# A graph layer and a mixture of experts on one core: where PSUM tiles share a bank, and the order of the work behind the edges

## The chip, the core and the metric

The kernel runs on one core of a Trainium2 chip. The core has a matrix engine (TensorE, PE in the rows; PEld is its weight load), a vector engine (VectorE, DVE), an activation engine (ScalarE, ACT), GpSimd (POOL), which here issues the indirect transfers, and SyncE (SP), which issues most other transfers. Each has its own instruction sequence and runs it in order; semaphores tie the sequences together. Matrix products land in PSUM, which is divided into banks; the framework gives each PSUM tile, and each buffer of a tile, a bank of its own. The metric is the time of one execution on the device, in microseconds.

## What is computed

There are 6250 nodes with 256 features and 100000 edges, sorted by their destination; the destinations are drawn so that low node numbers have many edges and high ones few. Everything is float32. Cut to what matters:

```python
x0 = layernorm(x); xn = layer_norm(x0, ln1_g, ln1_b)
h = (xn @ W).reshape(N, 8, 32)                   # 8 heads
e = leaky_relu(a_src[src] + a_dst[dst], 0.2)     # per edge (and self loop) and head
alpha = softmax of e over the edges of each destination
agg = segment_sum(h[src] * alpha, dst)
o = layer_norm(agg + xn @ W_res + bias, ln2_g, ln2_b)
x = x + o + (gelu_tanh(o @ ffn_w1 + ffn_b1) @ ffn_w2 + ffn_b2)     # 256 -> 1024 -> 256
t = layernorm(x)
# mixture of experts: 8 experts, each token goes to its best 2
w, idx = top-2 of softmax(t @ Wr + br), renormalised
y_e = gelu((norm(t) * ln_g[e] + ln_b[e]) @ W1[e] + b1[e]) @ W2[e] + b2[e]
x = x + sum over the 2 of w * y_e
```

## The kernel before

**First stage (to about 144 us).** Tiles of 128 nodes are normalised and turned, and give a table `tab_s` in DRAM (rows of `h` and two exponentials per head), tables of destination factors, and the accumulators `acc_lo` and `acc_hi` in SBUF. In this stage L724 writes the PSUM tile `ph` of 288 columns; L726 copies its first 256 columns on ACT into `hg`, and L727 adds a row to the last 32 on DVE into `abp`.

**Edge steps.** The edges are cut into 196 steps of 4 x 128 edges (`G` = 4). The steps run from the highest destinations to the lowest. A group of 1 to 8 steps shares a window of destinations; at high destinations a group is one step. What a step does is spread over seven places by `STAGES` (L922); the number is how many steps after the gather it is done, and the list's order is the order in which one step's work is issued: sum_up 6, weigh 3, add_tiles 4, place 4, turn_spread 1, give 2, spread 0, add_nodes 5, fetch 0. That is:

- fetch (POOL, L824): four gathers of rows of `tab_s` into `gs`, four buffers.
- spread (DVE, L833): one-hot rows `oh`; turn_spread (PE L846 into the tile `pt`, ACT L848): its transpose `oht`.
- give (PE L854): the factors of each edge's destination into `pz`, a tile of 64 columns with two buffers.
- weigh (DVE L862, L865, L866): `ww` is `gs` times `pz`, then the messages `msg`.
- add_tiles (PE L881): messages into `pl`; behind a group's last step ACT copies it to `part` (L885).
- add_nodes (PE L906, once a group): `part` into `p2`, a tile with one buffer; sum_up (DVE L917, twice): `p2` into `acc_lo` or `acc_hi`.

**Tasks between them.** All other work is written as tasks (L928 on): a function, an engine, a cost, tasks that it depends on with a gap in steps (1 step by default), and a PSUM tile that it takes and that a later task frees. The tasks stand in the list `pending`. In each step `run_tasks` (L949) goes through that list in order, again and again, and issues each task whose dependencies are met and whose engine has room left in that step: `ROOM` while there are edges (less what the edges take), `ROOM_AFTER` behind them. The order of all instructions is so fixed when the program is built; the waits between engines are then added by the framework from the tiles that the instructions read and write. The one tile `py` is held by one user at a time (the set `held`).

- first_product (L1157): `xn @ W_res` into `py`; add_biases (L1167, L1170) on DVE; stored to DRAM as `res_d` and `xp_d`.
- A node unit (L1193) is two tiles of 128 nodes: load_nodes (L1038, from `res_d` and `xp_d` into `res` and `xin`), divide, two norms, a net (next point), take_up (L1083), norm_new, store_new (L1106, SP), make_normed (L1119, ACT), logits (PE L1127 into `py`), choose (DVE L1135 on).
- A net (L1008): turn (PE L978 into `pt`, ACT L985 into `turned_in`); eight tasks up (L989), one for each 128 of the 1024 columns of the first layer: four matmuls (L993; a product of two halves of 128, each issued as two) into `ph`, a tile of 256 columns with two buffers, then the activation `ht` (ACT L996); then the tasks down (L999), up to 32 matmuls (L1003) into `py`.
- Each two node units make a chunk: mark, weight, count (PE L1286, L1287 into `py`), rank, enlist (all the expert blocks that are sure by now), scatter (POOL L1396: each token's row into `xs`, twice).
- Behind the chunk before the last, eight tasks clear (L1405, SP) write three rows of zeros per partition behind each expert's tokens, at a row that is read from `endi`. The framework puts them in order with each other and with the scatters, since all write `xs`.
- An expert block (L1504, L1521) is 256 rows of `xs` of one expert: load_weights (SP L1447 to L1449, 2 MB into two or three buffers), load_block (SP L1456), a net, finish (DVE L1488), weigh_block (ACT L1494), give_back (POOL L1498: an indirect transfer that adds to `out`, one for each 128 rows). There are 53 in the main loop: 50 whole and 3 half ones (numbers 50 to 52); `turn_of` is the order in which they run.

Of the kernel before, what the change touches and what calls it, by code (L numbers as in the profile page):

```python
# [45 lines left out]
F32 = mybir.dt.float32  # L46
# [8 lines left out]
P = 128  # L55
# [6 lines left out]
G = 4  # L62
# [7 lines left out]
BEHIND = {"PE": 0.5, "DVE": 1.4}  # L70
ROOM_AFTER = {"PE": 7.7, "DVE": 7.0, "ACT": 7.0, "POOL": 5.2, "SP": 1e9}

# [150 lines left out]
def gnn_moe_kernel(  # L223
# [28 lines left out]
    nc = tc.nc  # L252
# [10 lines left out]
    DA = D + H  # L263
# [42 lines left out]
    for i in range(NS - NF):  # L306
        turn_of += [NF + i, NF - (NS - NF) + i]
    turn_of += range(NS, NX)
# [483 lines left out]
    bps = edges.enter_context(tc.tile_pool(name="bps", bufs=1, space=PSUM))  # L792
    right = ctx.enter_context(ExitStack())

# [56 lines left out]
    def give(s):  # L851

        pz = bps.tile([P, G * 2 * H], F32, name="pz", bufs=2)
        nc.tensor.matmul(pz, live.pop((s, "oht")), live[order[s][0], "qd"].rearrange(  # L854
            "p j c -> p (j c)"), start=True, stop=True)
        live[s, "pz"] = pz
# [45 lines left out]
    @behind_group  # L902
    def add_nodes(q):
        part, oh2 = live.pop((q, "part")), live.pop((q, "oh2"))
        p2 = bps.tile([P, DA], F32, name="p2")
        nc.tensor.matmul(p2, oh2, part, start=True, stop=True)  # L906
        live[q, "p2"] = p2
# [32 lines left out]

    pending = []
    held = set()

    def task(*a, **k):
        t = Task(*a, **k)
        pending.append(t)
        return t

    def run_tasks(s, room):  # L949

        more = True
        while more:
            more = False
            for t in list(pending):
                if (t.take in held or room[t.eng] <= 0.0
                        or any(d.step is None or d.step + gap > s for d, gap in t.deps)):
                    continue
                pending.remove(t)
                t.step = s
                room[t.eng] -= t.cost  # L960
                if t.take:
                    held.add(t.take)
                if t.free:
                    held.remove(t.free)
                t.fn()
                more = True
# [22 lines left out]
    def up(c, env, w1, func, b):  # L989
        W = env["n"] * P  # L990
        ph = cps.tile([P, 2 * P], F32, name="ph", bufs=2)
        for k in range(KD):
            nc.tensor.matmul(ph[:, :W], w1[:, k, c * P:(c + 1) * P], env["in"][:, k, :W],  # L993
                             start=k == 0, stop=k == KD - 1)
        ht = cw.tile([P, 2 * P], F32, name="ht", bufs=2 * KF)
        nc.scalar.activation(ht[:, :W], ph[:, :W], func, bias=b[:, c:c + 1], scale=1.0)  # L996
        env["ht", c] = ht

    def down(j, c0, c1, env, w2):  # L999
        if j == 0 and c0 == 0:  # L1000
            env["py"] = cps.tile([P, 2, D], F32, name="py")
        for c in range(c0, c1):
            nc.tensor.matmul(env["py"][:, j, :], env["ht", c][:, j * P:(j + 1) * P], w2[:, c, :],  # L1003
                             start=c == 0, stop=c == KF - 1)

    turns, downs_, ups_ = [], [], []

    def net(env, src, deps, w1, w2, func, b, more=(), scale=None):  # L1008

        n = env["n"]  # L1010
        tn = task(lambda: turn(src(), "in", env, scale and scale()), "PE", 0.3 * n,
                  [*deps, *[(d, 0) for d in back(ups_, 2)]])
        free = [(d, 0) for d in back(downs_, 2)]
        ups = [task(lambda c=c: up(c, env, w1(), func, b()), "PE", 0.46 * n, [tn, *more, *free])
               for c in range(KF)]
        dn = []
        for j in range(n):
            for c in (0, KF // 2):
                dn.append(task(lambda j=j, c=c: down(j, c, c + KF // 2, env, w2()), "PE", 1.85,
                               [(dn[-1], 0)] if dn else [ups[-1]], take=None if dn else "py"))  # L1020
        turns.append(tn)
        ups_.append(ups[-1])
        downs_.append(dn[-1])
        return dn[-1]
# [98 lines left out]
    def logits(n, env):  # L1123
        pl = cps.tile([P, 2, D], F32, name="py")
        for j in range(n):
# [31 lines left out]
    def first_product(n, env):  # L1157
        py = cps.tile([P, 2, D], F32, name="py")
        for j in range(n):
# [21 lines left out]
    def first_unit(u):  # L1181
# [3 lines left out]
                                [(d, 0) for d in back(firsts, 2)]))  # L1185
        pr = task(lambda: first_product(n, env), "PE", 0.95 * n, [(first_loads[-1], 2)], take="py")
        ab = task(lambda: add_biases(n, env), "DVE", 0.7 * n,
                  [pr, *[(d, 0) for d in back(firsts, 1)]], free="py")
        firsts.append(task(lambda: store_first(t0, n, env), "SP", 0.0, [ab]))

    loads, turned, added, normed, chosen_, scattered = [], [], [], [], [], []

    def node_unit(u):  # L1193
        t0, n, _ = units[u]
        env = {"n": n}
        ld = task(lambda: load_nodes(t0, n, env), "SP", 0.0,
                  [(firsts[u], 0),
                   *[(d, 0) for d in back(turned, 2) + back(added, 2) + back(normed, 3)]])
        dv = task(lambda: divide(t0, n, env), "DVE", 0.85 * n, [ld])
        no = task(lambda: norm_out(n, env), "DVE", 0.6 * n + 1.9, [dv])  # L1200
# [4 lines left out]
                 scale=lambda: prm[:, PR_L2G:PR_L2G + 2 * KD])  # L1205
        tk = task(lambda: take_up(t0, n, env), "DVE", 0.35 * n, [dn, ao], free="py")
        nn = task(lambda: norm_new(t0, n, env), "DVE", 0.6 * n + 2.6,
                  [tk, *[(d, 0) for d in back(chosen_, 3)]])
        st = task(lambda: store_new(t0, n, env), "SP", 0.0, [tk])
        free = scattered[u - 4] + scattered[u - 3] if u >= 4 and u % 2 == 0 else []  # L1210
        mn = task(lambda: make_normed(n, env, u), "ACT", 0.55 * n,
                  [nn, (st, 0), *[(d, 0) for d in free]])
        tn = task(lambda: turn(env["xe"], "rt", env), "PE", 0.3 * n,
                  [mn, *[(d, 0) for d in back(chosen_, 2)]])
        lo = task(lambda: logits(n, env), "PE", 0.9 * n, [tn], take="py")
        ch = task(lambda: choose(t0, n, env), "DVE", 0.65 * n, [lo], free="py")
        loads.append(ld)
        turned.append(turns[-1])
# [64 lines left out]
    def count(env):  # L1283
        pr = cps.tile([P, 2, D], F32, name="py")
        m = env["m"].rearrange("p e t -> p (e t)")
# [102 lines left out]

    placed = {u: [] for u in range(NT)}
    between = cp.tile([P, 1], F32, name="between")  # L1390

    def scatter(u, j):
        t = units[u][0] + j
        n = rows(t)
        for k in range(2):
# [3 lines left out]
            tc.add_to_no_dep_group("slots", st.ins)  # L1399
            placed[u].append(st.ins)  # L1400
            tc.declare_no_dep(st.ins, group="slots", reason="each token has slots of its own")

            nc.gpsimd.memset(between, 0.0)

    def clear(e):  # L1405

        r = nc.sync.value_load(endi[0:1, e:e + 1], min_val=0, max_val=E * CAP - 3 * P)
        nc.sync.dma_start(xs[bass.ds(r, 3 * P), :].rearrange("(p r) d -> p r d", r=3),
                          blank[:, None, :].to_broadcast([P, 3, DX]))

    def chunk_tasks(us, final, before_final):
# [4 lines left out]
        ad = task(lambda: append(t0, n, env, us[0] // 2), "DVE", 1.0, [we])  # L1416
        co = task(lambda: count(env), "PE", 0.6, [mk], take="py")
        rk = task(lambda: rank(t0, n, env), "DVE", 2.6, [co], free="py")
        tok0 = chunked[0]
# [9 lines left out]
        for u in us:  # L1429
            scattered.append([task(lambda u=u, j=j: scatter(u, j), "POOL", 2.6,  # L1430
                                   [rk, ad, *[(d, 0) for d in cleared]])
                              for j in range(units[u][1])])
            sc += scattered[-1]
# [87 lines left out]
    def block_unit(b, env):  # L1521
# [6 lines left out]
        fi = task(lambda: finish(env), "DVE", 0.35 * n, [dn, *[(d, 0) for d in back(stored, 3)]],  # L1528
                  free="py")
        wb_ = task(lambda: weigh_block(env), "ACT", 0.45 * n, [fi, no])  # L1530
# [20 lines left out]
    final_list, there = [], None  # L1551
    s, u, since, was_nodes = 0, 0, [], False

    with tc.manual_schedule():
        nc.sync.dma_start(xs[E * CAP:, :].rearrange("(p r) d -> p r d", r=2),
                          blank[:, None, :].to_broadcast([P, 2, DX]))
        while s < NG + LASTST or pending or u < len(units) or len(blocks) < NS:
# [22 lines left out]
            while sum(t.cost for t in pending if t.eng == "PE") < QUEUE:  # L1580
                if (u < len(units) and units[u][2] <= s - LASTST
                        and not (ahead and was_nodes)):
                    was_nodes = True
                    node_unit(u)
                    since.append(u)
                    u += 1
                    if u % 2 == 0 or u == len(units):
                        chunk_tasks(since, u == len(units), u == len(units) - 1)
                        since = []
                elif ahead:  # L1590
                    was_nodes = False
# [54 lines left out]
```

## Time and profile before

| | |
|---|---|
| median of three runs | 1924.65 us (1918.36 to 1925.77) |
| the profiled execution | 1919.82 us; span of its instructions 1917.9 us |
| mean granted clock of PE over the span | 0.924 |
| busy: PE / DVE / ACT / POOL | 1614.6 / 1080.1 / 700.6 / 1124.8 us |
| moved by DMA | 347.86 MB, 181 GB/s on average |
| the two first-layer groups of L993 (experts, nodes) | 1696 and 800 matmuls, 386.5 and 194.1 us |
| ACT L996 (experts, nodes) | 424 and 200 activations, mean 468 and 470 ns |

How to read it. The page gives each engine's busy time, a strip of 40 slices of the span, a chain of work that ended last, and groups of like instructions with their busy time, the mean length of one and what ended the idle time in front of them. A row of a timeline is: start in us, length in us, engine, line, operation, what is written and read, how many; in brackets the idle time before it and what ended it. A row of waits reads "who waits <- for whom: us in total, times, longest". Matmuls run into each other, so a mean length of one (381 ns) is longer than the distance of two (about 218 ns, from 32 in 6.99 us).

### The profile page before, as it was taken

What the parts mean: (1) busy time and instruction counts of PE and PEld (TensorE: products, weight loads), DVE (VectorE), ACT (ScalarE), POOL (GpSimd) and SP (SyncE); (2) the same over time, 40 slices, a digit from 0 to 9 for tenths busy, and PEclk for the clock granted to TensorE, in tenths of its full rate; (3) what the DMA queues carried; (4) which work ended last, traced back from release to release, by engine and by line L of the source; (5) the groups of instructions that cost most, each with busy time, mean ns of one, the idle gap of its engine ahead of it and who ended that gap; (6) DMA issues with size and microseconds to landing.
All of it is one profiled execution on the core that took longest, in us unless ns stands there. A gap on an engine that the chain in (4) does not pass through costs nothing. (4 is left out here: it accounts for less than half of the span.)

```text
span 1917.9 us, 28185 instructions
## 1 busy us (share of the span) xinstructions
PE 1614.6 (84%) x8479; PEld 1238.1 (65%) x8479; DVE 1080.1 (56%) x3972; ACT 700.6 (37%) x1585; POOL 1124.8 (59%) x1162
## 2 busy tenths in 40 slices
PE   4835787878777899999799999999999996898996
PEld 3523565655555677776577777767777774676885
DVE  8836888877788757584755665546444351131010
ACT  3831233223222344344334434343434341442342
POOL 2027775755565767767677677777877772221222
PEclk8967899988877899999999999999999997998998
DMA  4967665554445476666565666767578674737671
GB/s 127 296 204 221 202 197 151 161 160 135 140 134 167 139 211 172 169 199 166 160 189 155 204 193 178 230 181 237 178 226 251 182 210 151 234 72 236 185 223 31
DMA packets 246622, 347.86 MB, mean 181 GB/s; under 512 B 46033, under 2 KB 202865, under 8 KB 246460
## 3 DMA queue, kind: packets, MB, share of 16 engines
q1 hardware_dynamic: 184268, 203.16, 32.7%
q0 software_dynamic: 58880, 139.32, 28.1%
q10 hardware_dynamic: 3312, 3.48, 0.6%
q8 instruction: 70, 1.15, 0.2%
q14 instruction: 92, 0.75, 0.1%
HBM read 282.50 MB, written 67.26 MB: 182 GB/s over the span
## 5 line engine op out<-in xcount | busy, mean ns | idle before, releaser
L824 POOL DMA_INDIRECT gs<-tab_s,srce x784 | 816.5, 1041 | 371.0 <-issue 201.6
L993 PE MATMUL ph<-turned_in,w1b 128*128 128x256 f32 (+1 forms) x1696 | 386.5, 381 | 35.0 <-DMA w1b<-in_L_ffn_W_dram 19.2
L1003 PE MATMUL py<-w2b,ht 128*128 128x256 f32 x1648 | 375.0, 386 | 14.3 <-DVE lg L1135 7.3
L993 PEld LDWEIGHTS ph<-turned_in,w1b 128*128 128x128 f32 x1696 | 300.5, 192 | 99.6 <-ACT ht L996 32.5
L1003 PEld LDWEIGHTS py<-w2b,ht 128*128 128x128 f32 x1648 | 316.1, 194 | 59.7 <-DVE lg L1135 8.9
L1498 POOL DMA_INDIRECT out_dram<-yb,tos x103 | 171.9, 1669 | 245.4 <-ACT yb L1494 125.3
L996 ACT ACTIVATE ht<-ph,pc 128x256 f32<-128x256 f32 (+1 forms) x424 | 196.5, 468 | 257.7 <-PE ph L993 255.5
L866 DVE TENSOR_TENSOR msg<-gs,msg 128x1024 f32<-128x1024 f32 x196 | 240.3, 1226 | 6.7
L993 PE MATMUL ph<-turned_in,w_sb 128*128 128x256 f32 (+1 forms) x800 | 194.1, 396 | 11.9 <-ACT ht L996 11.3
L1003 PE MATMUL py<-w_sb,ht 128*128 128x256 f32 x784 | 187.7, 400 | 11.2 <-DVE lg L1135 10.5
L1488 DVE TENSOR_TENSOR yb<-py,b2b 128x512 f32<-128x512 f32 (+1 forms) x53 | 35.8, 675 | 266.5 <-PE py L1003 252.9
L1003 PEld LDWEIGHTS py<-w_sb,ht 128*128 128x128 f32 x784 | 156.6, 202 | 38.9 <-DVE lg L1135 14.7
L993 PEld LDWEIGHTS ph<-turned_in,w_sb 128*128 128x128 f32 x800 | 151.7, 201 | 42.7 <-ACT ht L996 16.2
L848 ACT ACTIVATE oht<-pt 128x128 f32<-128x128 f32 x196 | 53.9, 275 | 288.5 <-PE pt L846 257.5
L885 ACT ACTIVATE part<-pl 128x264 f32<-128x264 f32 x110 | 42.9, 390 | 313.3 <-PE pl L881 310.3
L996 ACT ACTIVATE ht<-ph,prm 128x256 f32<-128x256 f32 (+1 forms) x200 | 92.8, 470 | 124.7 <-PE ph L993 124.4
L1396 POOL DMA_INDIRECT xs<-xe,slot x98 | 104.8, 1069 | 56.7 <-DMA xs<-blank 28.0
L881 PE MATMUL pl<-msg,oh 128*32 128x264 f32 x1568 | 131.1, 406 | 5.1 <-DVE msg L866 5.0
L906 PE MATMUL p<-part,oh 128*128 128x264 f32 x220 | 85.0, 472 | 55.3 <-DVE acc_hi L917 37.1
L862 DVE TENSOR_TENSOR ww<-gs,pz 128x64 f32<-128x64 f32 x196 | 42.1, 215 | 158.5 <-PE pz L854 100.3
L846 PEld LDWEIGHTS pt<-ident,oh 128*128 128x128 f32 x196 | 27.7, 141 | 139.0 <-issue 85.0
L917 DVE SCALAR_TENSOR_TENSOR acc_lo<-p,here,acc_lo 128x264 f32 x112 | 55.2, 493 | 101.1 <-PE p L906 79.6
(334 smaller groups left out, 1925.7 us busy)
## 6 DMA issues: line engine op xcount, KB each, us to landing
w1b<-in_L_ffn_W_dram SPq DMA_DIRECT2D x53, 1024.0 KB
w2b<-in_L_ffn_W_dram SPq DMA_DIRECT2D x53, 1024.0 KB
xb<-xs SPq DMA_DIRECT2D x50, 260.0 KB
gs<-tab_s,srce POOLq DMA_INDIRECT x784, 3.5
b2b<-in_L_ffn_b_dram SPq DMA_DIRECT2D x53, 128.0 KB
tab_s<-hg SPq DMA_DIRECT2D x12, 544.0 KB
xg<-in_x_dram SPq DMA_DIRECT2D x12, 512.0 KB
xt_d<-xt SPq DMA_DIRECT2D x12, 512.0 KB
```

Of the source, the lines that this page charges most:

```text
L824: nc.gpsimd.indirect_dma_start(out=gs[:, j, :], out_offset=None, in_=tab_s, in_offset=bass.IndirectOffsetOnAxis(ap=srce[:, t:t + 1], axis=0))
L848: nc.scalar.activation(oht, po[:, 0, :P], AF.Copy)
L866: nc.vector.tensor_tensor(msg[:, :, :D].rearrange("p t (h d) -> p t h d", h=H), gs[:, :, :D].rearrange("p t (h d) -> p t h d", h=H), msg[: ...
L881: nc.tensor.matmul(pl[j * W32:(j + 1) * W32, :], oh[:, j, :], msg[:, j, :], start=i == 0, stop=last)
L885: nc.scalar.activation(part, pl, AF.Copy)
L906: nc.tensor.matmul(p2, oh2, part, start=True, stop=True)
L917: nc.vector.scalar_tensor_tensor(to, p2, here[:, b, q:q + 1], to, op0=ALU.mult, op1=ALU.add)
L993: nc.tensor.matmul(ph[:, :W], w1[:, k, c * P:(c + 1) * P], env["in"][:, k, :W], start=k == 0, stop=k == KD - 1)
L996: nc.scalar.activation(ht[:, :W], ph[:, :W], func, bias=b[:, c:c + 1], scale=1.0)
L1003: nc.tensor.matmul(env["py"][:, j, :], env["ht", c][:, j * P:(j + 1) * P], w2[:, c, :], start=c == 0, stop=c == KF - 1)
L1396: st = nc.gpsimd.indirect_dma_start(out=xs, out_offset=bass.IndirectOffsetOnAxis(ap=slots[k][:n, t:t + 1], axis=0), in_=xes[u // 2][:n, pl ...
L1498: st = nc.gpsimd.indirect_dma_start(out=out, out_offset=bass.IndirectOffsetOnAxis(ap=tos[:, b, j:j + 1], axis=0), in_=env["yb"][:, j, :], ...
```

## The change

- `ROOM_AFTER`, the room of a step behind the edges, is halved.
- In `turn_of` each half block now comes behind a whole one in place of before it, so that the last block is a half one.
- `pz` is no longer a tile with two buffers but one half, by turns, of one tile `pzs`, and `ph` likewise of one tile `phs`. Each pair so lies in one bank, where it had two.
- `p2` has two buffers. `py` is now two tiles, `py0` and `py1`; a task takes the one that is spare, and frees it.
- A node unit's loads are made when the unit before it is made. Its store waits in the plan two steps behind take_up; make_normed no longer waits for the store's place in the plan, and scatter does.
- The tasks of the last node unit and of its chunk are put at the head of the list.
- The eight zero stores are no longer ordered with each other or with the scatters before them; the scatters after them wait for all of them.

```diff
-ROOM_AFTER = {"PE": 7.7, "DVE": 7.0, "ACT": 7.0, "POOL": 5.2, "SP": 1e9}
+ROOM_AFTER = {"PE": 3.9, "DVE": 3.5, "ACT": 3.5, "POOL": 2.6, "SP": 1e9}
...
     for i in range(NS - NF):
-        turn_of += [NF + i, NF - (NS - NF) + i]
+        turn_of += [NF - (NS - NF) + i, NF + i]
...
+    pzs = bps.tile([P, 2, G * 2 * H], F32, name="pzs")
...
     def give(s):
-        pz = bps.tile([P, G * 2 * H], F32, name="pz", bufs=2)
+        pz = pzs[:, s % 2, :]
...
-        p2 = bps.tile([P, DA], F32, name="p2")
+        p2 = bps.tile([P, DA], F32, name="p2", bufs=2)
...
+    spare = ["py0", "py1"]
     def task(*a, **k):
         t = Task(*a, **k)
-        pending.append(t)
+        if urgent:
+            pending.insert(urgent[0], t)
+            urgent[0] += 1
+        else:
+            pending.append(t)
...
-                if (t.take in held or room[t.eng] <= 0.0
+                if (t.take and not spare or room[t.eng] <= 0.0
...
                 if t.take:
-                    held.add(t.take)
+                    t.take["bank"] = spare.pop(0)
+                t.fn()
                 if t.free:
-                    held.remove(t.free)
-                t.fn()
+                    spare.append(t.free["bank"])
...
     def up(c, env, w1, func, b):
-        ph = cps.tile([P, 2 * P], F32, name="ph", bufs=2)
+        ph = phs[:, len(upped) % 2]
+        upped.append(c)
...
-            env["py"] = cps.tile([P, 2, D], F32, name="py")
+            env["py"] = cps.tile([P, 2, D], F32, name=env["bank"])
...
+    phs = cps.tile([P, 2, 2 * P], F32, name="phs")
...
+    def node_loads(u):
+        loads.append(task(lambda: load_nodes(t0, n, env), "SP", 0.0,
+                          [(firsts[u], 0), *[(d, 0) for d in back(turned, 2) + back(added, 2)
+                                             + back(normed, 3) + back(stores, 3)]]))
...
-        st = task(lambda: store_new(t0, n, env), "SP", 0.0, [tk])
+        stores.append(task(lambda: store_new(t0, n, env), "SP", 0.0, [(tk, 2)]))
         mn = task(lambda: make_normed(n, env, u), "ACT", 0.55 * n,
-                  [nn, (st, 0), *[(d, 0) for d in free]])
+                  [nn, *[(d, 0) for d in free]])
...
     def clear(e):
+        for i in blanks + [i for u in placed for i in placed[u]]:
+            tc.declare_no_dep(st.ins, i, reason="no rows of other tokens or experts")
+        blanks.append(st.ins)
...
                 if (u < len(units) and units[u][2] <= s - LASTST
                         and not (ahead and was_nodes)):
+                    if u == len(units) - 1:
+                        urgent.append(0)
+                    if u not in loaded:
+                        loaded[u] = node_loads(u)
-                    node_unit(u)
+                    node_unit(u, loaded[u])
                     since.append(u)
                     u += 1
+                    if u < min(len(units), len(firsts)):
+                        loaded[u] = node_loads(u)
```

## The prediction

> **What bounds the kernel now.** I read the page first, then the busy time of four stretches that I chose by what runs in them: 0 to 144 us builds the tables (the first gathers of L824 start near its end), 144 to 672 runs edges and node units (no expert block before 653 us), 672 to 1584 runs edges and expert blocks side by side, 1584 to 1918 is what is left when the edges are done. Columns: length, PE, weight loads, DVE, ACT, POOL, granted clock, DMA share, GB/s.
>
> ```profile
> PE 1614.6 (84%) x8479; PEld 1238.1 (65%) x8479; DVE 1080.1 (56%) x3972; ACT 700.6 (37%) x1585; POOL 1124.8 (59%) x1162
> ...
> 144.00:672.00 528.00, 410.15 (x2087) 296.48 (x2085) 417.95 (x1455) 147.96 (x342) 343.19 (x361) 0.84 0.56 164
> 672.00:1584.00 912.00, 844.70 (x4724) 651.51 (x4723) 517.31 (x1798) 366.95 (x793) 682.22 (x659) 0.98 0.67 194
> 1584.00:1918.00 334.00, 280.98 (x1338) 234.33 (x1336) 44.95 (x195) 110.70 (x242) 74.07 (x60) 0.93 0.55 162
> ```
>
> From 672 us on PE sets the pace: 845 of 912 us, then 281 of 334. Whatever lengthens PE's own sequence there lengthens the kernel. From 144 to 672 PE (410) and DVE (418) are about equal and wait for each other.
>
> Then the waits of PE from 144 to 672, because the change adds banks for `p2` and `py` (us in total, times, longest):
>
> ```profile
> PE p L906 <- DVE acc_hi L917: 37.1, 16, 5.7
> PE p L906 <- DVE acc_lo L917: 18.0, 6, 7.0
> PE py L1161 <- DVE rg L1167: 14.1, 9, 2.2
> ...
> PE py L1003 <- DVE lg L1135: 10.5, 7, 2.2
> ```
>
> This is what one bank costs: PE can't write the next result until DVE has read the last. 55.1 us stand at `p2`, 34.3 at `py` (the two rows above and six short kinds; one more wait of 12.4 us at the start of the stage is DVE's own wait for its first operands, and I count it as staying).
>
> **The column pairs (L992), the term that decides.** Now PE writes column c+1 of the first layer into one bank while ACT reads column c from the other. A run of seven columns in the timeline, PE and then ACT (start, duration):
>
> ```profile
> 1456.40 6.26 PE L993 MATMUL ph<-turned_in,w1b 128*128 128x256 f32 x28
> ...
> 1457.52 0.47 ACT L996 ACTIVATE ht<-ph,pc 128x256 f32<-128x256 f32 x1 [0.81 <-PE ph L993]
> 1458.38 0.47 ACT L996 ACTIVATE ht<-ph,pc 128x256 f32<-128x256 f32 x1 [0.39 <-PE ph L993]
> 1459.25 0.47 ACT L996 ACTIVATE ht<-ph,pc 128x256 f32<-128x256 f32 x1 [0.39 <-PE ph L993]
> ```
>
> A column takes PE 0.87 us (the spacing of the ACT rows), ACT starts 1.12 us after PE began and takes 0.47, all beside the next column. After the change both columns lie in one tile of one bank. Do the waits, which the framework places, keep halves of a bank apart? Before, no tile is written in one half while the other is read, but one is read by two engines at disjoint columns: L726 copies columns 0 to 255 of L724's `ph` on ACT, L727 adds to columns 256 to 287 on DVE. Neither needs the other's result.
>
> ```profile
> 96.79 0.38 ACT L726 ACTIVATE hg<-ph 128x256 f32<-128x256 f32 x1 [0.28 <-PE ph L724]
> ...
> 97.21 0.19 DVE L727 TENSOR_TENSOR abp<-ph,crow 128x32 f32<-128x32 f32 x1 [0.39 <-ACT hg L726]
> ```
>
> DVE waits for ACT to leave the bank (96.79 + 0.38 = 97.17, DVE at 97.21); that wait occurs 12 times, 7.0 us. So two engines on one bank are put in order even at disjoint columns, and I expect the same here: column c+1 waits for ACT's read of column c. Queued behind the waiting matmul is all of PE's sequence, edges included. PE resumes 0.06 us after ACT (an `ht` that began at 1575.00 and took 0.47 released PE at 1575.53). A column in a run then takes 1.12 + 0.47 + 0.06 = 1.65 us in place of 0.87: **0.78 more**. The bounds: 0 if halves are kept apart, 0.78 if not; I take 0.78, the row of L727 being nearest.
>
> How often: four matmuls are a column, so 104, 360 and 160 columns of L993 lie in the three stretches. Only a column that directly follows another pays. In the timeline of the middle stretch a net's eight columns stand mostly as 7 and 1, with edge work between; counting all runs, 80, 287 and 142 columns follow another. In the last stretch 28 of the 142 are of half width, where I take 0.46 (PE began at 1858.16 and ACT at 1858.80, 0.64; an `ht` 0.37, restart 0.06, less a spacing of 0.61). The price: 80 x 0.78 = 62, 287 x 0.78 = 224, 114 x 0.78 + 28 x 0.46 = 102 us.
>
> The Trainium skill, Perfetto Trace Analysis, Matmul Optimizations, asks that all 8 banks be used; by that rule alone these pairs cost nothing, since the freed banks are used again. The rows differ: a second bank is worth 0.78 us where PE and ACT alternate column by column.
>
> **The factors (L853).** `pz` loses its second bank too. In a step PE runs add_tiles, turn_spread, give, add_nodes; DVE runs sum_up, weigh. Give (s-2) must now wait for weigh (s-3) of the same step, which stands right behind sum_up on DVE. Before, add_nodes, the next thing on PE, waited for that sum_up. So the 55.1 us at `p2` do not go: the new `pz` wait takes their place, later by one L862 (0.22 us). What is late next is `pz`. From 672 us on DVE waits for PE's `pz` (100 us in 26 waits), so DVE is ahead and the wait costs nothing. Bounds: minus 55 to plus 16 (71 steps of 0.22 us); I take 0, since sum_up and L862 follow each other on DVE.
>
> **Two banks for results.** The 34 us at `py` go from 144 to 672, and 9.6 from 672 to 1584 (PE waits for `lg` and `pos`). A result no longer blocks others, so the planner can place more per step; PE's total work is the same, so behind 672 us I give nothing for it.
>
> **The end.** PE's worst pause:
>
> ```profile
> 1590.52 23.63 SPq L1408 DMA_DIRECT2D xs<-blank  x8
> ...
> 1625.40 9.25 PE L993 MATMUL ph<-turned_in,w1b 128*128 128x256 f32 x32 [19.16 <-DMA w1b<-in_L_ffn_W_dram]
> ```
>
> Eight zero stores, one after the other (3.2 us each), hold SP's queue, and behind them the next weights; PE stands for 19.2 us. Side by side, eight issues at about 1.2 us each (SP's pitch across a register load, 1616.87 to 1618.05) start when `endi` is there (1580.7) and end near 1590; the weights, 7.3 us to land, come before PE wants them at 1606. **Minus 19.2.** POOL's scatters, which wait for all zeros, start some 22 us earlier. The last node unit's loads ahead of time and its tasks put first take away the pauses for `yb` behind `res` (4.8) and `xb` (6.8). The matmuls after these three pauses ran slowly (9.25, 10.13 and 10.19 us against 7.16, 7.07 and 8.02): 7.4. A half block as the last one ends with one L1498 scatter in place of two (1904.89 to 1909.52): 4.6. Together 43; with shorter steps, which only reorder this stretch, and the weights as what is late next, I take 35. Bounds 0 and 43. Stores issued two steps later free SP (449 us of its waits), but PE waits for no weights before 1584: 0. That a scatter waits in the plan for its unit's store costs nothing either: both stand behind the count and the ranks, which take longer.
>
> **Sum**, on the profiled execution (1919.82 us, span 1917.9, 1.9 around it; the median of the three runs is 4.8 above it, and I leave that out):
> 144 to 672: 62 less 34 is 28; DVE's equal load hides about half of it: +14 (bounds 0 and 62).
> 672 to 1584: 224 - 10 = +214 (all cover is PE's own).
> From 1584: 102 - 35 = +67.
> 1917.9 + 295 + 1.9 = **2215 us**.
>
> **Clock.** Will PE's pauses of 0.5 us lower it? Around 296 to 304 us pauses of 0.53 and 2.03 us left it at 1.00; from 412 to 416, in a pause of 4.84, it was 0.50. So no. The Trainium skill (TensorE: Matmul & The Clock Gate, A second HAM failure mode) says that small idles between groups that cycle through PSUM can make the clock swing; if so, columns would go as in the row at 1625.40, with ACT starting 2.18 us after PE in place of 1.12, and 624 columns would add about 660 us.
>
> **Rivals.**
> *The halves are kept apart* (ends not slower). Place: the wait of L993 for L996; price 0; it decides below 0.12 us per column (the gains of 17 + 10 + 35 over 509 columns). Then 34/2 + 10 + 43 go, and half of the 55, since `pz` waits no more than before: 1920 - 97 = about 1825 us. For it: the diff alternates halves. Against: L727. 5%.
> *Half of the waits are filled*: with two result banks, other PE work falls between columns. Against: a step's tasks are placed in the order of the list, so ups stay together. For: runs of 7 and 1 show that steps cut nets. 2215 less half of 388 is about 2020 us. 8%.
> *The clock falls too*: price from rows, a slow column costs 1.06 us more (2.18 against 1.12): 2215 + 660 = 2875 us. Against: the rows above. 3%.
> *Forecast*: 84%, its own range 2075 to 2315. Below: the first stretch hides its 62 and all 43 are won at the end (-14, -8), the 68 us in which PE already stands in the middle stretch coincide with new waits, and shorter steps cut the last stretch's runs so that half of its 102 goes: 2215 - 14 - 8 - 68 - 51 = 2074. Above: DVE hides nothing (+48), nothing is won at the end (+35), and `pz` costs its 16: 2314.
>
> **Numbers.** The range leaves out the first and third rival and most of the second: 2075 to 2315. Faster by over 0.5% (about what a measurement of this kernel can tell from no change) 4%, within it 1%, slower 95%.
>
> **What would show it.** Right: PE waits for ACT `ht` at L993, several hundred times, 0.53 us each; ACT's `ht` spaced 1.65 in place of 0.87; the stretch with blocks longer by over 150 us; waits at L854 for DVE `ww` in place of those at L906; the `xs<-blank` rows overlapping and no 19 us pause. Wrong: `ht` still spaced 0.87, or waits at L993 without a longer span.

## The result and the profile after

Before: median 1921.5 us of 4 runs (1915.9 to 1925.8). After: 2286.7 us of 4 runs (2286.4 to 2294.6). The ratio is **1.191** (95% interval 1.189 to 1.194): the kernel became 365 us slower. The forecast was 2215 us with a range of 2075 to 2315; 72 us of the loss were not foreseen. The profiled execution after took 2294.6 us, with a span of 2292.8.

The page of the changed kernel, its busy times, and then three stretches, cut at the same events as those of before (144 us; 17 us after the first `ht` of an expert block, which came at 655.0 and now comes at 677.4; the end of the gathers). Columns of the stretches: length, PE, weight loads, DVE, ACT, POOL, granted clock, DMA share, GB/s.

```profile
PE 1762.7 (77%) x8479; PEld 1230.4 (54%) x8479; DVE 1079.1 (47%) x3972; ACT 701.5 (31%) x1583; POOL 1096.3 (48%) x1162
```

```profile
144.00:694.00 550.00, 413.35 (x2088) 283.59 (x2089) 418.64 (x1466) 150.25 (x345) 340.78 (x364) 0.88 0.55 162
694.00:1854.00 1160.00, 946.64 (x4684) 652.28 (x4685) 505.37 (x1740) 360.76 (x780) 659.03 (x656) 0.94 0.52 151
1854.00:2293.00 439.00, 325.26 (x1379) 239.96 (x1378) 57.14 (x250) 115.98 (x251) 71.47 (x59) 0.93 0.42 124
```

The stretches grew by 22, 248 and 105 us. The work did not: PE has the same 8479 matmuls, DVE the same 1079 us. But PE is busy 148 us longer with them, and its share of the span still fell from 84% to 77%: it both waits and works more slowly. In the middle stretch the granted clock fell from 0.98 to 0.94.

PE's wait for ACT at the first layer, before and then after, and its second largest wait after (us in total, times, longest):

```profile
PE ph L993 <- ACT ht L996: 27.1, 28, 1.8
```

```profile
PE phs L1000 <- ACT ht L1003: 306.2, 505, 3.0
PE pzs L855 <- DVE ww L863: 77.8, 29, 8.1
```

L1000 is the first layer's matmul, L1003 ACT's read of its column. The new wait occurs 505 times; 509 was foreseen. 46.3 us of it (81 waits) lie in the first stretch, 176.7 (286) in the second, 83.8 (139) in the third (one wait at a cut is in two of them). No wait at `p2` (L907) for DVE is left, and only 1.7 us at the results for DVE.

Two columns in the last stretch, PE, then ACT, then PE (start, duration, in brackets the idle time before and its releaser):

```profile
1893.42 1.13 PE L1000 MATMUL phs<-turned_in,w1b 128*128 128x256 f32 x4 [0.56 <-ACT ht L1003]
1894.59 0.47 ACT L1003 ACTIVATE ht<-phs,pc 128x256 f32<-128x256 f32 x1 [1.22 <-PE phs L1000]
1895.12 1.13 PE L1000 MATMUL phs<-turned_in,w1b 128*128 128x256 f32 x4 [0.56 <-ACT ht L1003]
```

PE and ACT take turns: 1.13 us of matmuls, ACT starts 1.17 after PE began, reads for 0.47, PE resumes 0.06 later. That is 1.70 us per column, against 0.87 before.

### The profile page after: what moved, and what is told of

Same layout as the page of the kernel before. It is cut to its first block, busy times and chain, and to the rows that moved or that the text cites. A ratio compares the mean times of both kernels' runs of the same rounds, so it can differ in the third digit from the quotient of the medians.

```text
span 2292.8 us, 28202 instructions
## 1 busy us (share of the span) xinstructions
PE 1762.7 (77%) x8479; PEld 1230.4 (54%) x8479; DVE 1079.1 (47%) x3972; ACT 701.5 (31%) x1583; POOL 1096.3 (48%) x1162
## 5 line engine op out<-in xcount | busy, mean ns | idle before, releaser
L825 POOL DMA_INDIRECT gs<-tab_s,srce x784 | 788.2, 1005 | 625.2 <-DVE msg L867 242.4
L1000 PE MATMUL phs<-turned_in,w1b 128*128 128x256 f32 (+1 forms) x1696 | 515.8, 431 | 214.0 <-ACT ht L1003 213.3
L1000 PEld LDWEIGHTS phs<-turned_in,w1b 128*128 128x128 f32 x1696 | 313.5, 207 | 394.1 <-ACT ht L1003 364.2
L1003 ACT ACTIVATE ht<-phs,pc 128x256 f32<-128x256 f32 (+1 forms) x424 | 198.2, 467 | 589.8 <-PE phs L1000 589.2
L1000 PE MATMUL phs<-turned_in,w_sb 128*128 128x256 f32 (+1 forms) x800 | 228.0, 409 | 92.9 <-ACT ht L1003 92.9
L1000 PEld LDWEIGHTS phs<-turned_in,w_sb 128*128 128x128 f32 x800 | 141.2, 196 | 168.7 <-ACT ht L1003 156.2
L1003 ACT ACTIVATE ht<-phs,prm 128x256 f32<-128x256 f32 (+1 forms) x200 | 93.8, 469 | 256.2 <-PE phs L1000 256.1
L863 DVE TENSOR_TENSOR ww<-gs,pzs 128x64 f32<-128x64 f32 x196 | 42.1, 215 | 270.8 <-PE pzs L855 254.7
L855 PE MATMUL pzs<-qd,oht 128*128 128x64 f32 x392 | 73.7, 272 | 77.9 <-DVE ww L863 77.8
L855 PEld LDWEIGHTS pzs<-qd,oht 128*128 128x128 f32 x392 | 73.5, 230 | 85.1 <-DVE ww L863 84.9
```

The lines of the kernel that those rows point to most:

```text
L825: nc.gpsimd.indirect_dma_start(out=gs[:, j, :], out_offset=None, in_=tab_s, in_offset=bass.IndirectOffsetOnAxis(ap=srce[:, t:t + 1], axis=0))
```

## The experiments

**Theory**: a pair of columns in one bank makes PE wait for ACT at each following column, and this is the whole loss; the other edits gain a little or nothing. **Rivals**: the factors' pair costs too, since its wait is now PE's second largest; or the edits behind the edges made the last stretch worse; or the clock, which fell, is a cost of its own.

Experiments 1 to 4 ran on one chip, 5 to 8 on a second, 9 to 11 on a third and 12 on a fourth, and each ratio is to the kernel before on the same chip. That matters here: on the chips of experiments 1 to 4 and 9 to 12 the kernel before took 2112 to 2117 us, on that of 5 to 8 1922, like in the result. So times are compared within a chip, and ratios across chips with care. All experiments compute the same outputs; number 6 adds products that nothing reads.

### 1. The change, with two banks for `ph`

```diff
-        ph = phs[:, len(upped) % 2]
-        upped.append(c)
+        ph = cps.tile([P, 2 * P], F32, name="ph", bufs=2)
...
-        p2 = bps.tile([P, DA], F32, name="p2", bufs=2)
+        p2 = bps.tile([P, DA], F32, name="p2")
```

> The changed kernel with the columns' tile given back its two banks (p2 goes back to one buffer to make room; the shared pz, the two result banks, the zeros, the steps and the order of the end stay). Theory (the columns' shared bank makes PE wait for ACT column by column, and the rest of the change gains): PE's waits at the first layer for ht, 306 us in the changed kernel, fall back to about 25; the time falls to 1840 to 1890 us, below the kernel before (1921). Rival (the loss comes from the other edits, the short steps, the new order, the shared factors): it stays above 2150 us.

Measured: 2083.7 us against 2114.8 before: 0.986 (0.982 to 0.990). PE's waits at `ph` for ACT fell to:

```profile
PE ph L999 <- ACT ht L1002: 53.2, 42, 7.4
```

The whole loss is gone, and a gain of 1.4% is left, a little less than the expected 1840 to 1890 us make against 1921 (0.958 to 0.984). The change itself did not run on this chip, but experiment 2 shows the loss there. The bank for `ph` came from `p2`, so the gain that is left doesn't need `p2`'s second bank.

### 2. The columns' pair alone

The kernel before, with `ph` as halves of one tile `phs`; nothing else.

```diff
-        ph = cps.tile([P, 2 * P], F32, name="ph", bufs=2)
+        ph = phs[:, len(upped) % 2]
+        upped.append(c)
```

> The kernel before with one edit: the columns' tile becomes two halves of one bank. Theory: 62 + 224 + 102 us on record for it, less what DVE hides in the first stretch, plus what the clock loses in the new pauses: 2270 to 2360 us, so as slow as the whole change or slower. Rival (other edits carry the loss): below 1960 us.

Measured: 2511.2 us against 2114.8: 1.185 (1.178 to 1.191), where the whole change has 1.191. Its first wait of PE:

```profile
PE phs L994 <- ACT ht L997: 316.5, 440, 8.2
```

One edit makes a loss of this size, as expected. That the ratio is almost that of the whole change may be chance: the change also has gains, and here the clock costs more. Its granted clock was 0.848, where the other three kernels on this chip had 0.897 to 0.902, and in its trace 133 of the spacings between full-width columns are about 2.64 us in place of 1.70. By 0.94 us each, some 125 of its 396 us are the clock's, an estimate.

### 3. The factors' pair alone

```diff
-        pz = bps.tile([P, G * 2 * H], F32, name="pz", bufs=2)
+        pz = pzs[:, s % 2, :]
```

> The kernel before with one edit: the factors' tile pz becomes two halves of one bank. Theory (the wait for the factors takes the place of the wait for p2, since sum_up and the reading of the factors follow each other on DVE): waits at p2 (55 us) all but vanish, waits at pz of 50 to 80 us appear, the time stays at 1915 to 1940 us. Rival (the factors' wait comes on top): 1960 us or more.

Measured: 2116.2 us, 1.001 (0.998 to 1.005). PE's waits:

```profile
PE pzs L854 <- DVE ww L862: 32.9, 16, 6.1
...
PE pzs L854 <- DVE acc_lo L917: 11.6, 2, 7.0
```

The wait is there, and its cost is within the interval of 0.5%: in this profile no wait of `p2` (L906) for DVE is left. Kernel 4, on the same chip and with both tiles as before, has 35.7 us of them, the largest being:

```profile
PE p L906 <- DVE acc_hi L917: 24.4, 10, 4.7
```

PE comes to a halt one operation earlier for the same DVE work.

### 4. The change, with all banks as before

Two buffers for `ph` and `pz`, one for `p2`, and one bank for results:

```diff
-    spare = ["py0", "py1"]
+    spare = ["py"]
```

What is left of the change is the earlier loads, the last node unit's tasks put first, the order of blocks, the short steps and the zero stores.

> The changed kernel with all of its banks as before (ph two, pz two, p2 one, one result bank): only the end's edits and the earlier loads are left. Theory: 19 us of the pause behind the zeros, and most of 43 in all, go: 1875 to 1890 us. The run with two result banks and the shared pz should be 10 to 35 us below this one if the result banks are worth what I gave for them; rival (the second result bank is worth nothing, since DVE sets the pace in the first stretch): the two are within 5 us, or this one is faster.

Measured: 2111.7 us, 0.999 (0.996 to 1.002): nothing, where 0.976 to 0.984 was expected (1875 to 1890 us against 1921). The timeline of SP, first in this kernel, then in kernel 3, which has the zero stores of before:

```profile
1801.90 10.50 SPq L1421 DMA_DIRECT2D xs<-blank  x8
```

```profile
1782.72 24.42 SPq L1408 DMA_DIRECT2D xs<-blank  x8
```

The stores do go side by side and hold the queue 10.5 us in place of 24.4. What PE waits for at a DMA, first in kernel 3, then in kernel 4:

```profile
PE ph L993 <- DMA w1b<-in_L_ffn_W_dram: 9.1, 1, 9.1
PE pt L978 <- DMA xb<-xs: 7.8, 2, 6.2
```

```profile
PE pt L983 <- DMA xb<-xs: 20.3, 1, 20.3
```

The pause for the weights is gone, and one for the rows `xb` of an expert block is there in its place: 16.9 us in kernel 3, 20.3 here. The stores' gain is lost to the transfer that is late next. All three kernels with these edits and one result bank (4, 10, 11) have this pause of 20 us, of the seven with two only kernel 5. Kernel 1 differs from this one by the second result bank and by the factors' pair, which cost nothing in kernel 3; it is 28 us faster (2083.7 us) and has no such pause. So most of what the second result bank is worth here may be this one pause; why the rows come later with one bank was not followed up.

### 5. The change, one wait for two columns

PE fills both halves of `phs`, then ACT reads both. Half as many waits, twice as long a run for each.

```diff
-            for k in range(KD):
-                nc.tensor.matmul(ph[:, :W], w1[:, k, c * P:(c + 1) * P], env["in"][:, k, :W],
-                                 start=k == 0, stop=k == KD - 1)
+        for i in (c, c + 1):
+            for k in range(KD):
+                nc.tensor.matmul(phs[:, i - c, :W], w1[:, k, i * P:(i + 1) * P],
+                                 env["in"][:, k, :W], start=k == 0, stop=k == KD - 1)
...
-        ups = [task(lambda c=c: up(c, env, w1(), func, b()), "PE", 0.46 * n, [tn, *more, *free])
-               for c in range(KF)]
+        ups = [task(lambda c=c: up(c, env, w1(), func, b()), "PE", 0.92 * n, [tn, *more, *free])
+               for c in range(0, KF, 2)]
```

> The changed kernel, but PE fills both halves of the columns' bank before ACT reads either, so there is one wait for two columns (a net has four tasks of two columns). Theory (PE stands while ACT is in the bank): a pair takes 0.87 + 1.15 for PE, two reads one behind the other 0.87, restart 0.06, so 2.95 us in place of 2 x 1.70, 0.22 less per column; over some 500 columns about 110 us: 2170 to 2200 us on a chip where the change takes 2287, ratio to the change 0.95. Rival (the cost is one of the wait itself, a fixed price for each time PE and ACT change places): half as many waits, half the cost, so 2090 or less, ratio 0.91.

Measured: 2114.1 us, 1.101 (1.097 to 1.105), 168 us below the change on the same chip (2282.0, experiment 8). PE's first wait, and two pairs in its timeline:

```profile
PE phs L999 <- ACT ht L1003: 198.6, 212, 2.1
```

```profile
1499.69 1.99 PE L999 MATMUL phs<-turned_in,w1b 128*128 128x256 f32 x8 [0.93 <-ACT ht L1003]
...
1502.62 1.99 PE L999 MATMUL phs<-turned_in,w1b 128*128 128x256 f32 x8 [0.93 <-ACT ht L1003]
```

The ratio to the change is 0.926, between the theory's 0.95 and the rival's 0.91, so neither had the size right. The rows decide: a pair takes 2.93 us, that is 1.19 more than two columns of before (2 x 0.87), where one wait of the change costs 0.83. The price of a wait is not fixed. 212 such waits are 252 us; 505 at 0.83 are 419; the difference, 167, is what was measured. (The expected gain was smaller, since I had counted more waits. That the two agree to 1 us is partly chance: this kernel has a pause of its own, 20.2 us for `xb`, and its clock, 0.931 over the span, is a little above the 0.926 of the change.) The loss goes with the number of waits times the price of one.

### 6. The change, its short pauses filled

Behind each column PE does one more product into a bank of its own that no one reads. It uses time in which PE would wait. `p2` has one buffer, for the bank.

```diff
+        nc.tensor.matmul(fill[:, :W], w1[:, 0, c * P:(c + 1) * P], env["in"][:, 0, :W],
+                         start=True, stop=True)
```

> The changed kernel with one more first-layer product behind each column, into a bank of its own that nothing reads (p2 has one buffer to make room; the outputs are the same): PE works 0.44 us of the 0.56 us in which it would stand. 624 added products of 0.44 us, of which nothing is needed. Theory (ten stretches of the changed kernel in which the clock stood at a half during runs of columns, 2.64 us a column in place of 1.69, come from the short pauses): with the pauses filled the clock stays near 1.00 in the runs and the time falls by 40 to 80 us, ratio to the change 0.965 to 0.985, though PE does more. Rival (the clock's falls have another cause, or cost nothing): the same time as the change or up to 30 us more, ratio 1.00 to 1.015.

Measured: 2273.4 us, 1.184 (1.180 to 1.188), against 2282.0 for the change. The clock rose from 0.926 to 0.958 over the span. In the middle stretch it rose from 0.95 to 1.00, first experiment 8, then this kernel (columns as in the stretches above):

```profile
694.00:1854.00 1160.00, 941.79 (x4724) 651.80 (x4722) 513.63 (x1772) 363.75 (x785) 658.54 (x658) 0.95 0.52 151
```

```profile
694.00:1854.00 1160.00, 1068.57 (x5480) 774.90 (x5480) 516.86 (x1774) 367.65 (x794) 657.24 (x659) 1.00 0.53 152
```

PE's wait for ACT fell from 306.1 us in 505 waits to:

```profile
PE phs L1000 <- ACT ht L1005: 45.4, 133, 2.5
```

The same columns at the same spacing of 1.70 us, but in experiment 8 40 of the full-width ones were spaced about 2.6 us (half clock), and here 2. So **short pauses did lower the clock**: the columns still take turns with ACT in one bank, and what the products change is that PE is not idle meanwhile. The time shows nothing of it: 0.996 of the change, with intervals that overlap, where 0.965 to 0.985 was expected. An estimate of why: 119 of the 624 products stand behind the last column of a run, where nothing was waited for, and at some 0.44 us each (a product's end behind the column's) they cost 52 us. The gain in time that I expected did not come; the gain in clock did.

### 7. Two banks where engines alternate, one where they don't

`ph`, the results and also `pt` (the turned tiles, which PE writes and ACT reads) have two banks; `pz` and `p2`, small and both behind the same DVE work, share one. The other edits as in the change.

```diff
-    pzs = bps.tile([P, 2, G * 2 * H], F32, name="pzs")
+    pzs = bps.tile([P, G * 2 * H + DA], F32, name="pzs")
...
-        pz = pzs[:, s % 2, :]
+        pz = pzs[:, :G * 2 * H]
...
-        p2 = bps.tile([P, DA], F32, name="p2", bufs=2)
+        p2 = pzs[:, G * 2 * H:]
...
-        pt = cps.tile([P, KD, 2 * P], F32, name="pt")
+        pt = cps.tile([P, KD, 2 * P], F32, name="pt", bufs=2)
...
-        ph = phs[:, len(upped) % 2]
+        ph = cps.tile([P, 2 * P], F32, name="ph", bufs=2)
```

> A version meant to beat both: the columns' tile has two banks, the results two, the factors and p2 share one bank (DVE reads both at the head of its step, so the one wait is there anyway), and the bank so freed goes to pt, the tile of the turns, where PE waits for ACT (44 us in the changed kernel, 36 in the one before). Theory (a second bank pays wherever PE and ACT take turns on the path): 15 to 40 us below the run with the columns' two banks, so a ratio of 0.965 to 0.98 to the kernel before. Rival (the wait only moves to the next ACT read, ACT being in order): within 8 us of that run, ratio 0.983 to 0.99.

Measured: **1832.3 us, 0.955 (0.952 to 0.958)**: faster than both kernels, and than the 0.965 to 0.98 expected, on the chip where before took 1921.7 and the change 2282.0. Its page, and its stretches with blocks and from the end of the gathers on:

```profile
PE 1594.5 (87%) x8479; PEld 1233.7 (67%) x8479; DVE 1079.6 (59%) x3972; ACT 691.0 (38%) x1583; POOL 1114.5 (61%) x1162
```

```profile
631.00:1532.00 901.00, 856.80 (x4814) 664.05 (x4810) 525.33 (x1813) 366.61 (x807) 683.72 (x670) 0.99 0.68 199
1532.00:1829.00 297.00, 271.39 (x1310) 227.38 (x1310) 49.33 (x216) 108.83 (x240) 73.03 (x60) 0.96 0.62 181
```

(The middle stretch begins here 2 us ahead of the first block's `ht`, which comes at 633.2.) What takes the place of the waits:

```profile
PE pzs L855 <- DVE ww L863: 111.6, 42, 8.2
```

The waits of `pt` for ACT's reads of the turned tiles (42.6 us before) fell to 1.7 us, no DMA stops PE at the end, and the last stretch has 297 us where before had 336 between the same events.

### 8 to 12. Repeats, and one bank for results

Experiment 8 is the change again, on the chip of 5 to 7:

> The changed kernel itself, as the measure for the two runs above on the same chip: ratio to the kernel before 1.18 to 1.20, as measured.

Measured: 2282.0 us, 1.189 (1.186 to 1.193). The loss is that of the result.

9 and 12 are kernel 1 again, 11 is kernel 4 again, and 10 is kernel 7 with `spare = ["py"]`; they were to split kernel 7's gain.

> The kernel of e1_ph_two_banks once more, because its first chip ran the kernel before at 2115 us; it differs from e7_turns_two_banks by the bank for the turns' tile pt alone (and p2 in its own bank). If this chip is like that of e7 (kernel before 1922): theory (44 us of waits at pt are worth about that where PE sets the pace): ratio to the kernel before 0.970 to 0.985, so 30 to 55 us above e7's 0.955. Rival (pt's bank is worth nothing, the fast chip alone makes the difference): 0.950 to 0.960.

> The kernel of e7_turns_two_banks with one result bank in place of two, nothing else. Theory (the 34 us at py in the first stretch are half hidden by DVE, and 10 us behind it count in full, and the last node unit waits for the one bank): 20 to 45 us slower than e7, ratio to the kernel before 0.965 to 0.978. Rival (the second result bank is worth nothing): 0.953 to 0.958.

> The kernel of e4_one_result_bank once more (all banks as before, only the end's edits and the earlier loads), for the same reason. There a pause of 20 us for xb stood where the kernel before had 6.8. Theory on record (35 of 43 us won at the end): ratio to the kernel before 0.98 to 0.985. Rival (with one result bank the last node unit comes late, so that the pause behind the zeros comes back as a pause for xb): 0.992 to 1.001 and a wait of PE for xb of 15 us or more.

> The kernel of e1_ph_two_banks a last time, in the hope of a chip on which the kernel before takes about 1922 us, as it did for the change and for e7_turns_two_banks. There: the prediction's own gains without the columns (17 + 10 + 35 = 62 us) make it 1858, ratio 0.968, and e7 (ratio 0.955) is then 25 us below it by the second bank of pt. Rival (pt's second bank is worth nothing): 0.952 to 0.958. Rival (the gains are not there, as on the other chip): 0.985 to 0.99, and then pt's bank alone made e7.

Measured: kernel 9: 2094.5 us, 0.990 (0.987 to 0.993). Kernel 10: 2090.8 us, 0.987 (0.982 to 0.991). Kernel 11: 2111.9 us, 0.996 (0.994 to 0.999). Kernel 12: 2091.3 us, 0.988 (0.983 to 0.993). The kernel before took 2117.1 beside 9 to 11 and 2112.2 beside 12, so none of these ran on a chip like that of kernel 7, and its 4.5% can't be split by them. Among themselves they say three things. The end's edits alone gain 0.1 and 0.4% (4 and 11). With the second result bank (and the factors' pair) on top, it is about 1% (1, 9 and 12): kernel 9 is 17 us faster than kernel 11, and kernel 11 has the pause for `xb`, 20.4 us, as its rival said. `pt`'s second bank with one result bank gains as much (10) as two result banks without it. How much of kernel 7's 4.5% is `pt`, the second result bank or the chip **stays open**.

## Why the prediction was right, and where it was too low

**The columns' wait: right.** That the framework orders PE's write behind ACT's read of the other half was argued from DVE and ACT at L726 and L727; the 505 waits show it, and kernels 1 and 2 show that it makes the loss. The Trainium skill, PSUM — Partial Sum Buffer, section "PSUM bank collisions raise a hardware error", has a rule that fits: guard PSUM by bank and partition quadrant, not by address. The halves differ in address alone, and the 505 waits agree; what the chip does without the wait no run here shows.

**Its price: 0.78 was 0.83.** The prediction let ACT start 1.12 us after PE began; alone, a column's four matmuls take 1.13 and ACT starts at 1.17. The other half of the picture is in PE's busy time: each wait is only about 0.56 us, but the four matmuls, which took 0.87 in a run, take 1.13 when nothing follows to overlap with; 0.56 + 0.26 is 0.82. 505 x 0.05 is 25 us of the miss.

**The clock: "So no" was wrong**, in about one column of ten. This is the step that failed in its mechanism. The prediction looked at two short pauses that left the clock at 1.00, and not at hundreds of them 1.7 us apart. The timeline after, PE alone:

```profile
729.80 1.13 PE L1000 MATMUL phs<-turned_in,w1b 128*128 128x256 f32 x4 [1.86 <-ACT ht L1003]
...
731.50 2.07 PE L1000 MATMUL phs<-turned_in,w1b 128*128 128x256 f32 x4 [0.56 <-ACT ht L1003]
...
734.13 2.07 PE L1000 MATMUL phs<-turned_in,w1b 128*128 128x256 f32 x4 [0.57 <-ACT ht L1003]
```

and the same place as stretches, the clock being the third number from the end:

```profile
724.00:732.00 8.00, 4.88 (x30) 3.25 (x29) 6.69 (x32) 6.02 (x12) 6.20 (x6) 0.96 0.83 281
732.00:744.00 12.00, 9.74 (x20) 5.37 (x18) 5.92 (x27) 1.90 (x4) 7.53 (x10) 0.50 0.43 131
744.00:752.00 8.00, 6.21 (x30) 3.58 (x29) 5.57 (x14) 3.46 (x6) 4.02 (x7) 0.93 0.58 195
```

The four matmuls go from 1.13 to 2.07 us, and the clock is 0.50 for 12 us with no pause over 1.9 us in the 10 us ahead. Some ten such episodes, most of them 12 to 20 us long, lie in runs of columns. Of the spacings of full-width `ht`, 53 are about 2.6 us; 53 x 0.94 (2.64 less 1.70) is 50 us. That is gross: in the kernel before, too, some matmuls of the first layer ran at half clock. On balance some 30 us of the miss are the clock's (the table below). The Trainium skill, TensorE: Matmul & The Clock Gate, section "A second HAM failure mode: psum-queue depth-cycling", says that small idles between groups that cycle through PSUM make the clock swing; the prediction weighed it and gave it all columns or none, 3%. These rows and kernel 6 agree with it, for a tenth of the columns; in kernel 2 it was about a quarter.

**The factors: right.** The `pz` wait takes the place of the one at `p2` at no cost that could be seen (kernel 3, 1.001). One pause, of 5.9 us, stands behind 672 us, where none was foreseen (the end, below).

**Results: right in kind.** The 34 us at `py` for DVE fell to 1.7. Apart, the second result bank was measured only together with the factors' pair and on slower chips: 28 us (kernels 1 and 4) and 17 us (9 and 11), and the pause of 20 us for `xb` is a part of both.

**The first stretch: 22 for 14.** The bounds were 0 and 62. In experiment 8 the first `ht` of a block came at 669.7, 15 us later than before, so two profiles of the changed kernel differ by as much as this one does from 14. That it was DVE that hid the rest fits, but was not shown apart.

**The end: about 13 for 35.** This term was mis-sized. (The three slow groups of matmuls in it also add up to 7.3 us, not 7.4.) The zero stores do go side by side in the changed kernel, and no pause for weights or `xb` is left there. Behind the gathers, PE's waits other than for `ht` fell from 34.7 to 14.6 us, which is 20 won; but PE also had 7 us more of other work left there, so 13 remain (the table below). Of the waits that are left, the longest single one stands ahead of the zero stores:

```profile
1872.24 0.69 PE L855 MATMUL pzs<-qd,oht 128*128 128x64 f32 x2 [5.94 <-DVE ww L863]
...
1874.78 11.70 SPq L1424 DMA_DIRECT2D xs<-blank  x8
...
1875.31 2.08 PE L1000 MATMUL phs<-turned_in,w1b 128*128 128x256 f32 x4 [0.56 <-ACT ht L1003]
```

After the pause of 5.94 us the whole next net, columns with their short pauses, goes at half clock until 1891. And the last half block saves nothing. POOL's scatters at the end, first before, then after:

```profile
1904.89 1.55 POOL L1498 DMA_INDIRECT out_dram<-yb,tos  x1 [5.71 <-ACT yb L1494]
1909.52 1.55 POOL L1498 DMA_INDIRECT out_dram<-yb,tos  x1 [3.08 <-DMA out_dram<-yb,tos]
```

```profile
2275.43 1.55 POOL L1517 DMA_INDIRECT out_dram<-yb,tos  x1 [17.98 <-ACT yb L1513]
2279.94 1.55 POOL L1517 DMA_INDIRECT out_dram<-yb,tos  x1 [2.96 <-DMA out_dram<-yb,tos]
2283.95 1.55 POOL L1517 DMA_INDIRECT out_dram<-yb,tos  x1 [2.46 <-DMA out_dram<-yb,tos]
```

The half block's scatter is one, but it queues behind the two of the whole block before it. With its columns free, kernel 7 wins 39 us in this stretch (297 for 336), though it has a `pz` pause there too (8.2 us); `pt`'s second bank may be a part of that, and a few matmuls less were left when the gathers ended. So a kernel without the columns' waits can reach some 35; in kernel 4 the pause moved to `xb`.

**The sum.** The profiled execution, the slowest of the four, was 375 us longer by its span, where 295 was foreseen. For each stretch, PE's waits for `ht` and the time of the first layer's matmuls are read from the two profiles, before and after; what they grew by is the columns' cost with the clock's part in it. The rest of a stretch's growth is what all other edits gained. In us:

| stretch | waits for `ht` | first-layer matmuls | columns: foreseen, measured | gains: foreseen, measured |
|---|---|---|---|---|
| first | 2.6, 46.3 | 103.1, 126.6 | 62, 67 | 48, 45 |
| with blocks | 20.9, 176.7 | 336.8, 441.2 | 224, 260 | 10, 12 |
| last | 3.5, 83.8 | 138.6, 176.0 | 102, 118 | 35, 13 |
| sum | | | 388, 445 | 93, 70 |

So of the 80 us that the profiled execution missed by, 57 are the columns' (25 by the price of a wait, about 30 by the clock, which is an estimate) and 23 are gains that did not come, at the end. The rival "halves kept apart" gave 1825 us for a change without the columns' waits; kernel 7 took 1832, but its banks are not the same, so that is a likeness and no proof. The rival "half of the waits are filled" fell: there were 505 waits for 509 columns. The forecast's range held because the mechanism and the count were right; with the price, the clock and the end all erring to one side, the time came within 30 us of its upper end.

## What to carry to other kernels

Count a PSUM bank by who takes turns at it: with waits placed as here, two halves of one bank are no double buffer between PE and its reader, however disjoint the columns. The same eight banks gave 2282 and 1832 us on one chip, by giving the pairs to the tiles where PE and a reader alternate within a microsecond (`ph`, results, `pt`), and one bank to tiles that wait for the same engine anyway. Most of the 450 us is `ph`: kernel 1, which gives `ph` alone its banks back, has 0.986 on its chip. The shares of the others are open. And price a wait in PE's sequence by more than its idle time: the matmuls beside it lose their overlap and, in some runs of such pauses, half of their clock.

## What the runs showed of the hardware

- With pauses of 0.56 us each 1.7 us the clock fell to 0.50 for 12 to 20 us at a time, in about a tenth of the columns (in kernel 2, on another chip, about a quarter); filling the pauses with products left 2 slow columns in place of 40 (kernels 8 and 6). What decides which runs of columns fall is not known from these runs.
- The same kernel before took 1922 us on some chips and 2112 to 2117 on others. In kernel 3's profile on such a chip PE stood 68 us, ACT 104 and DVE 85 in time that ends on nothing the profile shows, against 0, 15 and 29 in the first profile of before; kernel 1 has, for example, this row:

```profile
PE pt L847 <- issue: 38.3, 12, 20.1
```

What holds the engines there is not known from these runs. The ratio of the columns' pair alone (1.185) on one such chip is near that of the change (1.189, 1.191) on the others, with more of it the clock's; whether smaller gains, like that of kernel 7, carry over was not measured.
